# Four graph layers in one kernel: the seams between the passes rearranged

## The chip, the cores and the metric

The kernel runs on one core of one Trainium2 chip. Its time is the device time of one execution in microseconds; the time before is the median of three runs. The engines that matter are TensorE (PE in the profile; its weight loads are PEld), VectorE (DVE), ScalarE (ACT), GpSimd (POOL), SyncE (SP, here only a queue that issues transfers) and the DMA engines. A matmul in fp32 leaves two records in the trace, so four logical matmuls show as eight; a transpose leaves one.

## The reference

The input x has 128 batches of 128 nodes with 256 features, in fp32; adj is one 128 x 128 matrix. Four layers follow one another, each of the form x = x + f(relu(layernorm(x))):

```python
def layer(f, x):
    h = jnp.maximum(_layernorm(x, axis=-1), 0.0)
    return x + f(h)

# f of layer 0: two mixings of h by adj with gates and biases, and a gated loop; relu
# f of layer 1: causal attention within a batch, with adj as the additive mask
# f of layer 2: relu(adj @ (h @ W1)), relu(adj @ (. @ W2)), adj @ (. @ W3)
# f of layer 3:
agg = jnp.einsum('nm,bmd->bnd', A_hat, h)           # A_hat: adj normalised
x   = agg.reshape(-1, d)
z   = _batchnorm(x @ W1.T + b1, g1, be1)            # mean and variance over all 128 x 128 rows
out = jax.nn.relu(z) @ W2.T + b2
out = _batchnorm(out, g2, be2)                      # again over all rows
```

The two batch norms of layer 3 cut the kernel. Nothing after the first can start before the products with W1 of all batches are known, and nothing can be written out before the products with W2 of all batches are known.

## The kernel before

The batches are worked on in 32 groups of four. In the first pass the groups go through layers 0, 1, 2 and the first half of layer 3, staggered: while group g is in layer 2, group g+1 is in layer 1 and group g-1 in layer 3. A string of letters gives the order in which TensorE takes the pieces. The result z of a group (512 KB in two halves) is stored to device memory, but for the last group, which stays in SBUF. The residual x of every group is stored too. The second pass loads z back group by group, applies the first batch norm with relu on ScalarE, and multiplies with W2; the results of all groups stay in SBUF. The output stage applies the second batch norm, turns the result by transposes on TensorE, adds the residual (loaded ahead for some groups) and stores.

Most products are done in seven half-size products instead of eight (`seven`), which needs sums of operand quarters (VectorE) and copies of intermediate results (ScalarE):

```python
def sums(engine, a, extra, s3=None):
    a11, a12, a21, a22 = a
    ...
    engine.tensor_tensor(s1, a21, a22, ALU.add)
    engine.tensor_tensor(s2, s1, a11, ALU.subtract)
    engine.tensor_tensor(s4, a12, s2, ALU.subtract)
    engine.tensor_tensor(s3, a11, a21, ALU.subtract)
    return a11, a12, s4, a22, s1, s2, s3

def seven(product, put, shape, name, pool=None):
    px = bank(shape, f"{name}_x"); product(0, px, True);  t1 = kept(px, 1); yield
    py = bank(shape, f"{name}_y"); product(1, py, True);  put((0, 0), py, t1); yield
    pz = bank(shape, f"{name}_z"); product(4, pz, True);  t5 = kept(pz, 5); yield
    product(5, px, False); t2 = kept(px, 2); yield
    product(2, pz, False); put((0, 1), pz, t2); yield
    product(6, px, False); put((1, 1), px, t5); yield
    product(3, px, False); put((1, 0), px, None); yield
```

Layer 3 of a group in the first pass, and the seam between the passes:

```python
def layer3(g):
    h = norm(g, 3)
    yield
    gT = w.tile([P, DC, T], FP, tag="dT", name=f"gT_{g}", bufs=2)
    mixed(gT, h, ahT, f"pg_{g}", (nc.vector.tensor_copy,))
    ex = ...
    gs = sums(nc.vector, quarters_t(gT), ex)
    yield
    z = ZT[g] = [zp.tile([P, 2, T], FP, tag="z", name=f"zo_{g}_{j}") for j in range(2)]
    done = []

    def put(ij, pb, other):
        i, j = ij
        dst = z[j][:, :, i * T // 2 : (i + 1) * T // 2]
        if other is None:
            nc.scalar.copy(dst, pb)
        else:
            nc.vector.tensor_tensor(dst, pb, other, ALU.add)
        done.append(j)
        if done.count(j) == 2:
            for jj in range(2):
                nc.vector.bn_stats(stats1[:, 2 * j + jj, g, :], z[j][:, jj, :])
            if g != LAST:
                nc.sync.dma_start(Z[g][:, 2 * j : 2 * j + 2, :], z[j])

    yield from seven(columns_by_half(gs, SETS["b"], 0), put, [P, 2, T // 2], f"pz_{g}")

FINAL = "CCCCCCCCCCCCCCCCCCDCCDCCDdDDdDddDdDdddd"   # C: layer 2 of 31, D: layer 3 of 30, d: of 31
...
last1 = bn_part(stats1, FC, slice(LAST - 1, NG), "last1")
awake(60)            # 60 transposes of no use, that keep TensorE's clock up
passA.close()
...
sc1, sh1 = bn_affine(most1, last1, FC, g1_c, be1_c, "bn1", b1_c, 2)
```

`bn_affine` puts together the mean and variance of the first groups and of the last ones and makes a scale and a shift of them; its inverse square root is a power on GpSimd. `norm` takes statistics on VectorE, a power on GpSimd for a whole group, and a relu on ScalarE for each batch. Layer 2 of a group ends with two products `pr`, of two batches each, that are added to x; in layer 3 `mixed` makes the products `pg`.

The second pass and its buffers:

```python
OWN, IN_PASS, IN_Z, ROOM = 6, 8, 14, 19      # residual tiles ahead, by where they lie
...
for n, g in enumerate(ORDER):                # ORDER: the last group first
    ...                                      # relus, sums, seven products of group g
    if n + 1 + AT_ONCE < NG:
        load_z(n + 1 + AT_ONCE)
    if n % 4 == 3 and n // 4 < IN_PASS:
        load_x3(n // 4, nc.sync)
for g in range(IN_PASS, IN_Z):               # in the buffers of z, as they come free
    load_x3(g, nc.sync)
second_pass.close()
late = ...                                   # where the weights and sums of the pass were
for g in range(IN_Z, ROOM):
    load_x3(g, nc.sync)
...
for g in range(NG):
    x3 = R[g]
    for i in range(DC):
        nc.scalar.activation(O[g][:, i, :], O[g][:, i, :], AF.Identity, bias=..., scale=...)
    for q in range(G // 2):
        ...                                  # four transposes
        nc.vector.tensor_tensor(x3[:, half, :], pt, x3[:, half, :], ALU.add)
    nc.sync.dma_start(rows_out[g * P : (g + 1) * P], x3)     # the first and last in halves
    if g + ROOM < NG:
        load_x3(g + ROOM)                    # into a buffer whose store is done
```

Of the kernel before, what the change touches and what calls it, by code (L numbers as in the profile page):

```python
# [15 lines left out]
P = 128  # L16
# [6 lines left out]
def kernel(  # L23
# [55 lines left out]
    psum = ctx.enter_context(tc.tile_pool(name="psum", bufs=8, space=PSUM))  # L79

    def bank(shape, name):
        return psum.tile(shape, FP, tag="bank", name=name)
# [32 lines left out]
    passA = ExitStack()  # L115
# [34 lines left out]
    stats1 = weights.tile([P, FC, NG, 6], FP, name="stats1")  # L150
    stats2 = const.tile([P, DC, NG, 6], FP, name="stats2")
# [123 lines left out]
    def prepare():  # L275
# [57 lines left out]
        yield  # L333
        SETS["b"] = seven_of(bw1T, "bw1T")
# [22 lines left out]
    def norm(g, layer, bs=ALL):  # L357
# [19 lines left out]
        for k, b in enumerate(bs):  # L377
            nc.scalar.activation(  # L378
                h[:, b, :], xt[:, b, :], AF.Relu, bias=sh[:, k : k + 1], scale=rs[:, k : k + 1]
            )  # L380
        return h
# [385 lines left out]
    def layer3(g):  # L767

        h = norm(g, 3)
        yield  # L770
        gT = w.tile([P, DC, T], FP, tag="dT", name=f"gT_{g}", bufs=2)
        mixed(gT, h, ahT, f"pg_{g}", (nc.vector.tensor_copy,))
        ex = w.tile([P, 3, 1, T // 2], FP, tag="ex", name=f"gs_{g}", bufs=2)
        gs = sums(nc.vector, quarters_t(gT), ex)
        yield
# [3 lines left out]
        def put(ij, pb, other):  # L779
            i, j = ij  # L780
            dst = z[j][:, :, i * T // 2 : (i + 1) * T // 2]
            if other is None:
                nc.scalar.copy(dst, pb)
            else:
                nc.vector.tensor_tensor(dst, pb, other, ALU.add)
            done.append(j)
            if done.count(j) == 2:
                for jj in range(2):
                    nc.vector.bn_stats(stats1[:, 2 * j + jj, g, :], z[j][:, jj, :])
                if g != LAST:  # L790
                    nc.sync.dma_start(Z[g][:, 2 * j : 2 * j + 2, :], z[j])

        yield from seven(columns_by_half(gs, SETS["b"], 0), put, [P, 2, T // 2], f"pz_{g}")
# [14 lines left out]
    FINAL = "CCCCCCCCCCCCCCCCCCDCCDCCDdDDdDddDdDdddd"  # L808
# [40 lines left out]
    last1 = bn_part(stats1, FC, slice(LAST - 1, NG), "last1")  # L849
    awake(60)  # L850
    passA.close()

    def bn_affine(most, last, nch, gam, bet, name, bias, n):
# [4 lines left out]
        d = const.tile([P, nch], FP, name=f"d_{name}")  # L858
        nc.vector.tensor_tensor(d, mean1, mean, ALU.subtract)
        nc.vector.scalar_tensor_tensor(mean, d, share, mean, ALU.mult, ALU.add)  # L860
        nc.vector.tensor_tensor(mean, mean, bias, ALU.add)
        nc.vector.scalar_tensor_tensor(d, d, share * (1.0 - share), d, ALU.mult, ALU.mult)
        nc.vector.scalar_tensor_tensor(d, var, 1.0 - share, d, ALU.mult, ALU.add)
        nc.vector.scalar_tensor_tensor(var, var1, share, d, ALU.mult, ALU.add)
        sc = const.tile([P, nch], FP, name=f"sc_{name}")
        inv_sqrt(sc, var, BN_EPS)
        nc.vector.tensor_tensor(sc, sc, gam, ALU.mult)
        sh = const.tile([P, nch], FP, name=f"sh_{name}")
        nc.vector.tensor_tensor(sh, mean, sc, ALU.mult)
        nc.vector.tensor_tensor(sh, bet, sh, ALU.subtract)  # L870
        part = const.tile([P, nch], FP, name=f"part_{name}")
        nc.vector.tensor_tensor(part, bias, sc, ALU.mult)
        nc.vector.tensor_tensor(sh, sh, part, ALU.add)
# [3 lines left out]

    keep = ctx.enter_context(tc.tile_pool(name="keep", bufs=1, reuse_waits="tile"))
    O = [keep.tile([P, DC, T], FP, name=f"o_{g}") for g in range(NG)]


    OWN, IN_PASS, IN_Z, ROOM = 6, 8, 14, 19
    x3p = ctx.enter_context(tc.tile_pool(name="x3p", bufs=OWN, reuse_waits="tile"))
    zin = ctx.enter_context(
        tc.tile_pool(name="zin", bufs=3, side="right", reuse_waits="tile")
    )
# [8 lines left out]
    ORDER = [LAST, *range(LAST)]  # L895
# [8 lines left out]
    def load_x3(g, queue=nc.gpsimd):  # L904
# [5 lines left out]
        else:  # L910
            pool, tag = (x3p, "x3") if k < OWN else (zp, "z") if k < IN_PASS else (late, "x3l")
# [5 lines left out]
    def tell():  # L917

        for g, j in TOLD:
            tc.keep_in_program_order(  # L920
                nc.vector.bn_stats(stats2[:, j, (g + 1) % NG, :], O[g][:, j, :])
            )
        TOLD.clear()
# [4 lines left out]
    def second(g):  # L928

        zl, zr = ZT[g]  # L930
        ex = zw.tile([P, 2, FC // 2, T // 2], FP, tag="zs", name=f"zs_{g}")
# [28 lines left out]
        def put(ij, pb, other):  # L960
            i, j = ij
            dst = O[g][:, j, i * T // 2 : (i + 1) * T // 2]
            if other is None:
                nc.scalar.copy(dst, pb)
            else:
                in_order(dst, pb, other, ALU.add)
            done.append(j)
            if done.count(j) == 2:
                TOLD.append((g, j))
# [13 lines left out]
    for n, g in enumerate(ORDER):  # L983
# [14 lines left out]
        if n % 4 == 3 and n // 4 < IN_PASS:  # L998
            load_x3(n // 4, nc.sync)
    for g in range(IN_PASS, IN_Z):  # L1000
# [5 lines left out]
    late = ctx.enter_context(tc.tile_pool(name="late", bufs=ROOM - IN_Z, side="right", reuse_waits="tile"))  # L1006

    for g in range(IN_Z, ROOM):
        load_x3(g, nc.sync)
    tell()  # L1010
    last2 = bn_part(stats2, DC, slice(LAST, NG), "last2")
    sc2, sh2 = bn_affine(most2, last2, DC, g2_c, be2_c, "bn2", b2_c, 1)
    rows_out = out.rearrange("b (k r) d -> (b k) r d", r=G)
    for g in range(NG):
        x3 = R[g]
        for i in range(DC):
            nc.scalar.activation(
                O[g][:, i, :], O[g][:, i, :], AF.Identity,
                bias=sh2[:, i : i + 1], scale=sc2[:, i : i + 1],
            )  # L1020
        for q in range(G // 2):
            pt = bank([P, 2, D], f"pto_{g}_{q}")
            for r in range(2):
                for i in range(DC):
                    every = O[g][:, i, :].rearrange("c (p r) -> c p r", r=G)
# [45 lines left out]
```

## Time and profile before

| what | before |
|---|---|
| time, median of 3 (lowest to highest) | 2591.45 us (2590.89 to 2592.26) |
| span of the profiled run | 2589.5 us |
| first pass, to the last product with W1 | about 2315 us |
| filler on TensorE between the passes | 60 transposes, 6.7 us |
| second pass, products with W2 | 2321.6 to 2517.8 us |
| output stage, from the first activation | 2522.05 to 2589.5 us |
| moved in all | 143.07 MB |

The profile is one execution. A row of a timeline gives the start in us, the duration, the engine, the line of the kernel, the operation with what it writes and reads, and in square brackets how long the engine had been idle and what ended that. A row of windows gives a stretch of time, and for each engine how long it was busy in it. TensorE counts as busy while it does filler, so its share says little at the seam.

### The profile page before, as it was taken

The numbers are of one execution on the slowest core, as the hardware profiler recorded it, in microseconds if no ns is written. First come the engines' busy times: TensorE is split into PE (matmuls) and PEld (weight loads), VectorE is DVE, ScalarE is ACT, GpSimd is POOL, SyncE is SP. The second block draws the span as 40 slices with busy tenths as digits, with TensorE's granted clock in tenths as the row PEclk, the third lists the DMA queues.
The fourth block names the chain that finished last, engine by engine and source line by source line (L and its number), as shares of the span: only waits on it lengthen the run. The fifth ranks groups of instructions, "written<-read, shape, count | busy, mean of one in ns | idle before, by whom it ended". The sixth has DMA issues, their size and how long they took to land.

```text
span 2589.5 us, 40769 instructions
## 1 busy us (share of the span) xinstructions
PE 2536.8 (98%) x15331; PEld 2292.7 (89%) x15331; DVE 1907.7 (74%) x4788; ACT 1288.9 (50%) x2576; POOL 290.1 (11%) x566
## 2 busy tenths in 40 slices
PE   7999999999999999999999999999999999999996
PEld 5999999999999999999999999999999999888875
DVE  6777777777777777777777777777777776558876
ACT  4544445444444554444444445544454444337766
POOL 1111011111111111011111110111111111000001
PEclk9999999999999999999999999999999999999998
DMA  3000000000000000000000000000000000035559
GB/s 134 15 34 33 33 33 25 25 33 34 33 26 25 33 33 33 33 33 24 26 33 34 33 25 26 33 33 33 34 33 17 34 25 25 25 119 196 171 186 390
DMA packets 49656, 143.07 MB, mean 55 GB/s; under 512 B 4258, under 2 KB 23220, under 8 KB 45492
## 3 DMA queue, kind: packets, MB, share of 16 engines
q1 hardware_dynamic: 42740, 116.81, 12.4%
q0 software_dynamic: 6576, 23.60, 2.5%
q8 instruction: 121, 1.98, 0.3%
q14 instruction: 75, 0.61, 0.1%
q10 hardware_dynamic: 144, 0.07, 0.0%
HBM read 73.48 MB, written 66.98 MB: 54 GB/s over the span
## 4 chain that ended last, share of the span: by engine, by line
PE 94%; DVE 2%; DMA 1%; ACT 1%; POOL 0%; issue 0%; SPq 0%; DVEq 0%; POOLq 0%
PE p_x L446 17%; PE p_x L429 9%; PE p_z L446 8%; PE pmu L401 4%; PE p_z L429 4%; PE pz_x L446 4%; PE p_y L446 4%; PE po_x L951 4%; PE pu_x L429 4%; PE pg L401 2%; PE ps L630 2%; PE pm L555 2%; PE p_y L429 2%; PE pqv_x L587 2%; PE pr L760 2%; PE pz_z L446 2%
## 5 line engine op out<-in xcount | busy, mean ns | idle before, releaser
L378 ACT ACTIVATE h<-x,sh,rs 128x256 f32<-128x256 f32 x512 | 268.9, 589 | 359.3 <-POOL sh L372 349.7
L446 PE MATMUL p_x<-uT,w 128*128 128x256 f32 x1024 | 242.2, 379 | 0.0
L732 ACT ACTIVATE h2T<-h2T 128x512 f32<-128x512 f32 x192 | 120.6, 628 | 230.1 <-DVE h2T L731 230.1
L446 PEld LDWEIGHTS p_x<-uT,w 128*128 128x128 f32 x1024 | 189.7, 190 | 23.2
L363 DVE BATCH_NORM_STATS2 st<-x 128x6 f32<-128x256 f32 x512 | 191.1, 414 | 2.3
L369 POOL TENSOR_SCALAR rs<-mv 128x4 f32<-128x4 f32 x125 | 30.0, 240 | 1351.1 <-ACT h2T L732 1060.7
L513 DVE SCALAR_TENSOR_TENSOR gs<-h,gw 128x256 f32<-128x256 f32 x360 | 151.0, 420 | 27.9 <-ACT h L378 22.6
L461 ACT COPY p_t<-p_x 128x512 f32<-128x512 f32 (+1 forms) x192 | 96.8, 504 | 109.6 <-PE p_x L446 102.8
L370 POOL TENSOR_TENSOR rs<-rs,nhalf 128x4 f32<-128x4 f32 x125 | 145.2, 1161 | 0.0
L401 PEld LDWEIGHTS pmu<-a2T,u 128*128 128x128 f32 x1024 | 119.3, 192 | 14.8 <-issue 14.8
L429 PEld LDWEIGHTS p_x<-w,h2T 128*128 128x128 f32 x1024 | 124.3, 192 | 3.3
L685 ACT ACTIVATE u<-u 128x512 f32<-128x512 f32 x93 | 58.6, 631 | 133.9 <-DVE u L684 133.9
L429 PE MATMUL p_x<-w,h2T 128*128 128x128 f32 x1024 | 124.6, 275 | 0.0
L446 PE MATMUL p_x<-us,w_s 128*128 128x256 f32 x512 | 121.2, 379 | 0.0
L446 PE MATMUL p_x<-uT,w_s 128*128 128x256 f32 x512 | 121.1, 379 | 0.0
L446 PE MATMUL p_z<-us,w 128*128 128x256 f32 x512 | 121.0, 379 | 0.0
L446 PE MATMUL p_z<-us,w_s 128*128 128x256 f32 x512 | 121.0, 379 | 0.0
L446 PE MATMUL p_y<-uT,w 128*128 128x256 f32 x512 | 120.9, 379 | 0.0
L401 PE MATMUL pmu<-a2T,u 128*128 128x128 f32 x1024 | 119.5, 275 | 0.0
L761 DVE TENSOR_TENSOR x<-pr,x 128x512 f32<-128x512 f32 x64 | 43.7, 683 | 90.4 <-PE pr L760 90.4
L446 PEld LDWEIGHTS p_z<-us,w 128*128 128x128 f32 x512 | 97.3, 190 | 13.2
L446 PEld LDWEIGHTS p_z<-us,w_s 128*128 128x128 f32 x512 | 97.3, 190 | 13.2
(317 smaller groups left out, 6174.1 us busy)
## 6 DMA issues: line engine op xcount, KB each, us to landing
z<-zo SPq DMA_DIRECT2D x62, 512.0 KB, 2.6
zi<-z SPq DMA_DIRECT2D x31, 1024.0 KB, 4.9
x<-x POOLq DMA_DIRECT2D x32, 512.0 KB, 3.4
x<-in_x_dram SPq DMA_DIRECT2D x31, 512.0 KB, 4.1
out_dram<-x3i SPq DMA_DIRECT2D x30, 512.0 KB, 12.1
x3i<-x SPq DMA_DIRECT2D x19, 512.0 KB, 5.2
x3i<-x POOLq DMA_DIRECT2D x13, 512.0 KB, 11.1
w<-in_L_gnn_W_dram SPq DMA_DIRECT2D x1, 2048.0 KB
```

Source lines behind the costliest of these rows:

```text
L363: nc.vector.bn_stats(st[:, k, :], xt[:, b, :])
L370: nc.gpsimd.tensor_tensor(rs, rs, nhalf[:, :n], ALU.pow)
L378: nc.scalar.activation(h[:, b, :], xt[:, b, :], AF.Relu, bias=sh[:, k : k + 1], scale=rs[:, k : k + 1])
L401: nc.tensor.matmul(pm[:, k, :], src[:, b, c * P : (c + 1) * P], aT, start=True, stop=True)
L429: nc.tensor.matmul(pb[:, rr, :], a_r[r][:, c, rr * P : (rr + 1) * P], b_r[r][:, c, :wide], start=(first and rr == 0 and c == 0), stop=(c = ...
L446: nc.tensor.matmul(pb[:, jj, :], b_r[r][:, c, at : at + P], a_r[r][:, c, :], start=(first and jj == 0 and c == 0), stop=(c == nk - 1), ski ...
L461: nc.scalar.copy(t, pb)
L513: nc.vector.scalar_tensor_tensor(gs, h[:, b, :], 1.0, gw[:, i, :], ALU.mult, ALU.mult, accum_out=gl[:, k, i : i + 1],)
L555: nc.tensor.matmul(pm[:, r, :], cmbT[:, b, :], h[:, b, :], start=True, stop=True)
L685: nc.scalar.activation(dst, dst, AF.Relu)
L732: nc.scalar.activation(dst, dst, AF.Relu)
L951: nc.tensor.matmul(pb, BW2R[r][:, c, :], a_r[r][:, c, :], start=(first and c == 0), stop=(c == FC // 2 - 1), skip_group_check=True,)
```

## The change

It has five parts. The last group goes through layer 3 in two halves of two batches, each with a norm of its own (the power of two batches is asked for by VectorE), and its product with W1 is a plain one of four blocks, without sums and kept copies; its statistics, and those of the group before it, are taken for each half block, straight from PSUM where the result is not a sum. The last word of the order string moves one piece of group 30 behind layer 2 of group 31. `bn_affine` is written so that fewer steps lie before and after the power. The last result of the second pass stays in PSUM, which sets free 4 KB per partition for one more residual tile; the sums of the second pass get buffers that the residuals can take over while the pass still runs; nine residuals instead of eight are loaded within it. And the relus of the second group in layer 0 are pinned behind the instructions that come before them in the program. What it is for: a shorter way from the last product of one pass to the first of the next, fewer loads left for the output stage, and a start without a blocked queue.

```diff
+    passA = ExitStack()
+    psum = [passA.enter_context(tc.tile_pool(name="psum", bufs=8, space=PSUM))]
...
+    bw1T_12 = weights.tile([P, F1 // 2], FP, name="bw1T_12")
...
+        nc.scalar.copy(bw1T_12, bw1T[:, 0, F1 // 2 :])
         SETS["b"] = seven_of(bw1T, "bw1T")
...
-            nc.scalar.activation(
+            relu = nc.scalar.activation(
                 h[:, b, :], xt[:, b, :], AF.Relu, bias=sh[:, k : k + 1], scale=rs[:, k : k + 1]
             )
+            if (g, layer) == (1, 0):
+                tc.keep_in_program_order(relu)
...
     def layer3(g):
-        h = norm(g, 3)
-        yield
-        gT = w.tile([P, DC, T], FP, tag="dT", name=f"gT_{g}", bufs=2)
-        mixed(gT, h, ahT, f"pg_{g}", (nc.vector.tensor_copy,))
-        ...
+        parts = [ALL] if g < LAST else HALVES
+        for bs in parts:
+            h = norm(g, 3, bs)
+            yield
+        gT = tile_of(g, parts[0], [P, DC, T], "dT", f"gT_{g}", 2)
+        for i, bs in enumerate(parts):
+            mixed(gT, h, ahT, f"pg_{g}_{i}", (nc.vector.tensor_copy,), bs)
+            if g < LAST:
+                ...  # sums, as before
+            yield
...
         def put(ij, pb, other):
+            if other is not None:
+                nc.vector.tensor_tensor(dst, pb, other, ALU.add)
+            if g >= LAST - 1:
+                at = 2 * g - LAST + 1 + i
+                for jj in range(2):
+                    nc.vector.bn_stats(
+                        stats1[:, 2 * j + jj, at, :], (pb if other is None else dst)[:, jj, :]
+                    )
             if other is None:
                 nc.scalar.copy(dst, pb)
...
+        if g < LAST:
+            yield from seven(columns_by_half(gs, SETS["b"], 0), put, [P, 2, T // 2], f"pz_{g}")
+            return
+        for i, j in (0, 0), (1, 0), (0, 1), (1, 1):
+            pb = bank([P, 2, T // 2], f"pz_{g}_{i}_{j}")
+            for jj in range(2):
+                for c in range(DC):
+                    ...  # b: weights of block j, jj, chunk c
+                    nc.tensor.matmul(pb[:, jj, :], b, gT[:, c, i * T // 2 : (i + 1) * T // 2], ...)
+            put((i, j), pb, None)
+            yield
...
-    FINAL = "CCCCCCCCCCCCCCCCCCDCCDCCDdDDdDddDdDdddd"
+    FINAL = "CCCCCCCCCCCCCCCCCCDCCCCDDdDDddDdDdDdddd"
...
-    awake(60)
+    awake(41)
...
     def bn_affine(most, last, nch, gam, bet, name, bias, n):
+        nc.vector.tensor_scalar(var, var, 1.0 - share, BN_EPS, ALU.mult, ALU.add)
         nc.vector.tensor_tensor(d, mean1, mean, ALU.subtract)
+        nc.vector.scalar_tensor_tensor(var, var1, share, var, ALU.mult, ALU.add)
+        nc.vector.scalar_tensor_tensor(e, d, share * (1.0 - share), d, ALU.mult, ALU.mult)
+        nc.vector.tensor_tensor(var, var, e, ALU.add)
+        inv_sqrt(sc, var, 0.0)
         nc.vector.scalar_tensor_tensor(mean, d, share, mean, ALU.mult, ALU.add)
         nc.vector.tensor_tensor(mean, mean, bias, ALU.add)
-        ...  # four steps, inv_sqrt, and six steps
+        nc.vector.tensor_tensor(d, bias, mean, ALU.subtract)
         nc.vector.tensor_tensor(sc, sc, gam, ALU.mult)
+        nc.vector.tensor_tensor(sh, d, sc, ALU.mult)
+        nc.vector.tensor_tensor(sh, sh, bet, ALU.add)
...
-    OWN, IN_PASS, IN_Z, ROOM = 6, 8, 14, 19
+    psum.append(... tc.tile_pool(name="psum2", bufs=6, space=PSUM, reuse_waits="tile"))
+    last_o = ... tc.tile_pool(name="last_o", bufs=1, space=PSUM, reuse_waits="tile")
+    # O[ORDER[-1]]: two tiles of last_o; the other results in SBUF as before
+    OWN, IN_PASS, IN_Z, IN_ZS, ROOM = 7, 9, 15, 17, 20
+    zsp = ctx.enter_context(tc.tile_pool(name="zsp", bufs=2, side="right", reuse_waits="tile"))
...
-        ex = zw.tile([P, 2, FC // 2, T // 2], FP, tag="zs", name=f"zs_{g}")
+        ex = zsp.tile([P, 2, FC // 2, T // 2], FP, tag="zs", name=f"zs_{g}")
...  # put of the second pass, for the last group only:
+            told = stats2[:, j, LAST + i, :]
+                if last:
+                    tc.keep_in_program_order(nc.vector.bn_stats(told, pb))
                 nc.scalar.copy(dst, pb)
+                if last:
+                    TOLD.append((told, dst))     # statistics of the half, taken a step later
...
-        if n % 4 == 3 and n // 4 < IN_PASS:
-            load_x3(n // 4, nc.sync)
-    for g in range(IN_PASS, IN_Z):
+        if n % 3 == 2 and n // 3 < IN_PASS:
+            load_x3(n // 3, nc.sync)
+    for g in (9, 10, 15, 11, 12, 16, 13, 14):
         load_x3(g, nc.sync)
...
-    for g in range(IN_Z, ROOM):
+    for g in range(IN_ZS, ROOM):
         load_x3(g, nc.sync)
```

## The prediction

> **What bounds the kernel now.** I read the page first, then the timeline wherever TensorE is not back to back, then short windows of the end.
>
> ```profile
> PE 2536.8 (98%) x15331; PEld 2292.7 (89%) x15331; DVE 1907.7 (74%) x4788; ACT 1288.9 (50%) x2576; POOL 290.1 (11%) x566
> PE 94%; DVE 2%; DMA 1%; ACT 1%; POOL 0%; issue 0%; SPq 0%; DVEq 0%; POOLq 0%
> ```
>
> TensorE is on 94% of the chain that ended last, so what the change can win lies in the gaps of TensorE: the start, the seam between the two passes, the end. The start, from the timelines of ScalarE and TensorE (start, duration, instruction, what ended the idle time):
>
> ```profile
> 36.21 1.09 ACT L378 ACTIVATE h<-x,sh,rs 128x256 f32<-128x256 f32 x2 [3.64 <-POOL sh L372]
> 37.21 0.35 ACT L394 COPY hT<-pt 128x256 f32<-128x256 f32 x1
> 37.61 2.08 PE L606 MATMUL pqv<-hT,m_qk 128*128 128x256 f32 x4 [4.44 <-ACT hT L394]
> 40.92 1.03 PE L606 MATMUL pqv<-hT,m_qk 128*128 128x256 f32 x4
> 44.69 0.40 ACT L643 ACTIVATE p<-p,nmax 128x128 f32<-128x128 f32 x1 [1.68 <-DVE nmax L640]
> ```
>
> Two relus of group 1 stand in ScalarE's queue ahead of the copy of hT and wait for GpSimd until 36.21. The copy is blocked behind them, and TensorE with it for 4.44 us; its next four matmuls then take twice their usual time. The seam, from the timeline of all engines:
>
> ```profile
> 2297.09 1.88 PE L760 MATMUL pr<-s,a2T 128*128 128x512 f32 x4
> 2303.79 2.07 ACT L378 ACTIVATE h<-x,sh,rs 128x256 f32<-128x256 f32 x4 [1.61 <-POOL sh L372]
> 2315.06 6.71 PE L108 MATMUL awake<-ident 128*128 128x128 f32 x60
> 2315.88 1.29 DVE L789 BATCH_NORM_STATS2 stats<-zo 128x6 f32<-128x512 f32 x2 [0.28 <-ACT zo L783]
> 2318.76 1.01 POOL L221 TENSOR_TENSOR sc_bn<-sc_bn,nhalf 128x4 f32<-128x4 f32 x1 [15.00 <-DVE sc_bn L219]
> 2320.66 2.93 ACT L939 ACTIVATE zo<-zo,sh_bn,sc_bn 128x512 f32<-128x512 f32 x4 [4.81 <-DVE sh_bn L873]
> 2321.61 1.32 PE L951 MATMUL po_x<-zo,bw2T 128*128 128x256 f32 x4
> ```
>
> From the last real product (end about 2315.1) to the first of the second pass (2321.6), TensorE only does filler. The end, in windows (busy time of PE, PEld, DVE, ACT, POOL; then clock, DMA share, GB/s):
>
> ```profile
> 2512.00:2516.00 4.00, 3.91 (x18) 2.74 (x16) 3.96 (x8) 0.75 (x2) 0.00 (x0) 1.00 0.78 266
> 2516.00:2520.00 4.00, 1.32 (x5) 0.68 (x4) 3.08 (x12) 0.37 (x1) 0.00 (x0) 1.00 0.28 72
> 2520.00:2524.00 4.00, 1.09 (x4) 0.70 (x5) 1.06 (x8) 1.96 (x3) 0.70 (x1) 0.76 1.00 372
> 2580.00:2584.00 4.00, 0.00 (x0) 0.00 (x0) 0.00 (x0) 0.00 (x0) 0.00 (x0) 0.50 1.02 419
> 2584.00:2588.00 4.00, 0.00 (x0) 0.00 (x0) 0.00 (x0) 0.00 (x0) 0.00 (x0) 0.50 0.58 227
> ```
>
> The last compute instruction ends at about 2572, yet the DMA engines are full from 2520 to 2586. The end is bound by bytes: it is set by how much has still to move when the second pass frees its buffers.
>
> **What the Trainium skill says.** "TensorE: Matmul & The Clock Gate", Part 1, says that an idle window of about 3.4 us halves TensorE's clock; the trace agrees (2.08 against 1.03 us after the 4.44 us gap). "PSUM — Partial Sum Buffer", Engine vs sequencer instructions, says that ScalarE's and VectorE's queues are strict FIFO: that is the blocked copy. The same page, PSUM bank collisions, says that two engines may not touch one bank and partition quadrant at once, reads included; in the changed program each ScalarE copy of a PSUM result accordingly waits for VectorE's statistics of it. No run so far shows what that costs. "DMA: Bandwidth & Descriptors", Issuing engines are not separate DMA queues, says that all queues share 16 engines; the trace has share 1.02 at 419 GB/s whichever queue issues.
>
> **The change part by part.** I compared the order of instructions per engine. Between the first 80 us and the last group nothing moves but one added ScalarE copy of 128x256 (0.37 us beside full matmuls, 0). Times below are on the clock of before.
>
> *Start.* The copy of hT now comes before all four relus. Its transposes end at 33.2, VectorE's half of the copy at 34.1, so the projections run from about 34.1, warm, to 37.2 (1.76 us for each of two blocks; the first matmul is earlier). But the four relus still wait for 36.2, end at 38.3, and now the copy of qv stands behind them: 38.9. Then the exp table (1.28) and the first exp at 40.25 instead of 44.69. The exps gate the rest, so the gain is 4.4, kept to the end because TensorE is full from there.
>
> *Seam, removed.* pr_0 is issued before the last product of layer 2: 2294.45 instead of 2297.09. The norm of the first half follows: add 2295.5, two statistics and aggregates to 2297.25, power on GpSimd to 2298.2, relus 2298.45 to 2299.5 (before: all four from 2303.79). The second half still hangs on pr_1 (2298.8): add 2299.7, statistics 2300.7, power 2301.6, relus 2301.85 to 2304.05 with two copies between them. So pg of half 0 is not waited for, and pg of half 1 hardly.
>
> *Seam, added.* The plain product is 16 logical matmuls instead of 14; at two records each of 0.216 us (a product of 14 takes 6.04 us, 28 records) that is 0.86 us more on TensorE. TensorE from pr_0: pr 1.76, the layer-2 product 1.79, seven products of group 30 6.04, pg 1.79, plain blocks 6.90, sum 18.3, and about 1.0 of waiting (pr_1 waits for a ScalarE copy): end at 2313.7, 1.35 earlier.
>
> *Seam, the statistics.* Read from PSUM at 0.42 us each, they end 1.05 after the last product, at 2314.75 (before: copy, then 1.29 us of statistics, 2317.17). Aggregates to 2315.1; four small operations instead of six before the power (0.7) 2315.85; power 1.1; 2316.95; three after it 0.6; relu 2317.6; first product at its usual 0.9 later: 2318.5 instead of 2321.6. Seam: 3.1. ScalarE's copies, held by the statistics and by the store of group 30's z (2.6 us to landing), end about 2315.4, two us ahead of the relu. The filler, 41 x 0.109 (6.55 / 60) = 4.5 us, ends at 2318.2 and delays nothing.
>
> *Second pass.* 6.04 us per group of 28 records, as before; six PSUM banks are two groups of three. 0.
>
> *End of the pass, added.* VectorE gets one statistics of a half (0.37), one scaling (0.17) and a second half statistics (0.36) ahead of the add that releases the last product: that product starts 0.9 later and ends at 2518.75. After it, statistics from PSUM 0.4, aggregate 0.2, four operations 0.7, power 0.8, three 0.6: first output activation at 2521.45, 0.6 earlier than 2522.05. That is not what counts; the start of the last loads is.
>
> *Loads.* Before, 8 residual tiles are loaded in the pass, 4 at its end, 7 once it is over, 13 into reused buffers: after the pass 20 loads and 32 stores of 0.524 MB, 27.3 MB, which at 412 GB/s is 66.2 us: 2520 to 2586. After: 9 in the pass, 6 at its end (two in buffers of the sums), 5 once it is over, 12 reused: 49 instead of 52 transfers. 3 x 0.524 / 0.419 = 3.75 us less, 0.9 later: 2.85.
>
> Sum: 4.4 + 3.1 + 2.85 = 10.35; 2591.45 - 10.35 = 2581.1.
>
> **The rivals.** (a) *The end stays bound by bytes but starves at its beginning*: five loads instead of seven bridge the time to the first store. They last 7 us from 2520.2, the first store comes at 2524.7 (3.25 after the first activation, as before), so for is the arithmetic, against it that ScalarE gives one group per 1.41 us, 372 GB/s, under the 419. Cost up to 1 us: 2582. (b) *A late VectorE eats the seam*: statistics of half blocks are more instructions (0.42 twice against 0.69), and copies wait for them. VectorE has 2 us spare there; if not, 1 to 2 us of the 3.1 are lost: 2583. (c) *The wait at the start only moves*: the relus now delay qv. I have that in; were the exps not the gate, the gain would be the 3.5 us of hT alone: 2582. (d) *More than counted*: if the end of the pass doesn't slip by 0.9: 2580.
>
> **Range and chances.** The parts are independent and each is uncertain by about 1 us, the end by 1.5; all three are wins in working and none is large. Range 2578.0 to 2585.5. 2% is 52 us, far outside: faster 0.01, same 0.985, slower 0.005.
>
> **What would show it.** In the changed profile: no idle of 4 us ahead of the projection at 34, no slow matmuls there, exp at 40.2; filler of 41 followed by po_x within 0.5 us, 7.5 us (4.4 + 3.1) before 2321.6; DMA share at 1 from the end of the pass for about 62.5 us. Wrong would be: a shift at 100 us under 3.5, a relu of the seam that waits for something other than the last statistics, or DMA share under 0.9 within the end.

## The result and the profile after

| | before | after |
|---|---|---|
| time, median (lowest to highest) | 2591.17 us (2590.89 to 2592.26) | 2582.2 us (2580.38 to 2582.89) |
| ratio to before | | 0.9964, 95% interval 0.9946 to 0.9981 |
| span of the profiled run | 2589.5 us | 2581.1 us |

The kernel is 9.0 us faster; the interval of the ratio makes that 4.9 to 14.0 us. 2581.1 was predicted, with a gain of 10.35. A second measurement of the same kernel, further down, gave 0.9971. The page of the profile after (busy time of each engine; then the shares of the chain that ended last):

```profile
PE 2535.9 (98%) x15316; PEld 2293.4 (89%) x15316; DVE 1905.8 (74%) x4795; ACT 1288.8 (50%) x2577; POOL 288.9 (11%) x563
PE 95%; ACT 2%; DVE 1%; DMA 1%; issue 0%; POOL 0%; SPq 0%; DVEq 0%; POOLq 0%
```

Nothing of the 8.4 us between the two spans is visible there: TensorE is busy for 0.9 us less and no share of the chain moves by more than a point. The places have to be read one by one. The start, in the timelines of TensorE and ScalarE after (start, duration, instruction, what ended the idle time before it):

```profile
30.97 2.08 PE L612 MATMUL pqv<-hT,m_qk 128*128 128x256 f32 x4
36.13 0.37 ACT L400 COPY hT<-pt 128x256 f32<-128x256 f32 x1 [0.42 <-PE pt L398]
36.56 1.13 PE L612 MATMUL pqv<-hT,m_qk 128*128 128x256 f32 x4 [0.24 <-ACT hT L400]
37.21 2.08 ACT L381 ACTIVATE h<-x,sh,rs 128x256 f32<-128x256 f32 x4 [0.70 <-POOL sh L375]
42.18 0.41 ACT L649 ACTIVATE p<-p,nmax 128x128 f32<-128x128 f32 x1 [1.12 <-DVE nmax L646]
```

The order is the one the pin asks for. The copy of hT is no longer behind the relus, TensorE waits 0.24 us for it where it waited 4.44, and the four relus come after it. But the first exp is at 42.18, only 2.51 us ahead of before, and the slow projection (2.08 us) has not gone: it now comes first, at 30.97. The seam, from the timeline of all engines after:

```profile
2292.28 1.02 PE L766 MATMUL pr<-s,a2T 128*128 128x512 f32 x2
2296.68 1.09 ACT L381 ACTIVATE h<-x,sh,rs 128x256 f32<-128x256 f32 x2 [1.18 <-DVE sh L378]
2306.15 5.34 PE L820 MATMUL pz<-gT,bw1T 128*128 128x256 f32 x24
2311.33 4.64 PE L109 MATMUL awake<-ident 128*128 128x128 f32 x41
2311.53 0.76 DVE L798 BATCH_NORM_STATS2 stats<-pz 128x6 f32<-128x256 f32 x2 [0.96 <-PE pz L820]
2312.32 0.59 ACT L802 COPY zo<-pz 128x512 f32<-128x512 f32 x1 [0.41 <-DVE stats L798]
2314.95 2.93 ACT L983 ACTIVATE zo<-zo,sh_bn,sc_bn 128x512 f32<-128x512 f32 x4 [2.04 <-DVE sh_bn L902]
2316.07 1.15 PE L995 MATMUL po_x<-zo,bw2T 128*128 128x256 f32 x4
```

From the start of the filler to the first product of the second pass there are 4.74 us, where there were 6.55. The last statistics end 0.96 us after the last product, the relu of the second pass waits for the last step of the shift on VectorE, and the copies that had to wait for the statistics (0.41 us the last one) end at 2312.91, two us before the relu. The end, in windows (PE, PEld, DVE, ACT, POOL; then clock, DMA share, GB/s):

```profile
2512.00:2516.00 4.00, 1.04 (x4) 0.59 (x4) 2.46 (x14) 0.61 (x2) 0.70 (x1) 0.84 0.48 132
2516.00:2520.00 4.00, 3.39 (x15) 3.01 (x16) 1.36 (x3) 4.00 (x7) 0.00 (x0) 0.50 1.02 401
2524.00:2528.00 4.00, 3.45 (x24) 2.89 (x23) 3.89 (x8) 4.00 (x7) 1.65 (x3) 1.00 1.00 310
2572.00:2576.00 4.00, 0.00 (x0) 0.00 (x0) 0.00 (x0) 0.00 (x0) 0.00 (x0) 0.50 1.03 420
2576.00:2580.00 4.00, 0.00 (x0) 0.00 (x0) 0.00 (x0) 0.00 (x0) 0.00 (x0) 0.50 0.50 195
```

The DMA engines are full from 2516 to about 2578, while the last compute instruction is done well before: it is still bytes that set the end.

To compare traces that are shifted against each other, I read six marks in each: VectorE's first use of a weight matrix w that it has to wait for, the last product pm of group 0's layer 0 before group 1 starts (near 26 us), the first product pmu (near 130), the first po_x of the second pass, the last po_x of it, and the end. The first two columns are times from the start of the span, each of the next four is the distance to the mark before it, in us:

| kernel | w used | pm | pm to pmu | pmu to po_x | to the last po_x | to the end | span |
|---|---|---|---|---|---|---|---|
| before | 12.58 | 25.05 | 106.54 | 2190.02 | 195.10 | 72.8 | 2589.5 |
| after | 13.62 | 26.94 | 102.28 | 2186.85 | 195.84 | 69.2 | 2581.1 |
| after, again | 13.95 | 26.80 | 103.55 | 2186.85 | 195.85 | 69.3 | 2582.4 |
| without the pin | 13.91 | 27.21 | 105.89 | 2187.27 | 195.85 | 68.5 | 2584.7 |
| pin alone | 13.84 | 26.64 | 103.57 | 2190.28 | 195.10 | 72.7 | 2588.3 |
| last group whole, filler 60 | 14.06 | 27.27 | 102.23 | 2191.14 | 194.62 | 69.2 | 2584.5 |
| last group whole, filler 41 | 13.36 | 27.07 | 103.42 | 2189.46 | 195.55 | 69.0 | 2584.5 |
| two tiles fewer | 14.08 | 26.55 | 101.91 | 2187.23 | 195.85 | 71.6 | 2583.1 |
| statistics after the add | 14.50 | 27.55 | 102.08 | 2186.77 | 195.41 | 69.8 | 2581.6 |
| and early aggregate | 13.80 | 26.35 | 101.41 | 2187.29 | 193.90 | 69.8 | 2578.7 |
| without late loads | 14.46 | 27.80 | 102.28 | 2186.76 | 195.84 | 55.6 | 2568.3 |
| warm start | 14.47 | 27.61 | 102.05 | 2188.48 | 194.69 | 69.0 | 2581.8 |
| early aggregate, warm start | 14.39 | 27.90 | 102.10 | 2187.10 | 194.10 | 69.9 | 2581.1 |
| early aggregate, weights first | 14.01 | 27.02 | 102.04 | 2186.76 | 194.45 | 69.4 | 2579.7 |

Between before and after, 3.17 us go at the seam (3.1 predicted), 3.6 at the end (3.75 predicted), the pass grows by 0.74 (0.9 predicted). Of the 4.4 at the start the trace shows 4.26 from pm on, but pm itself is 1.89 us later than before. That is the question which the experiments had to settle.

### The profile page after: what moved, and what is told of

It reads as the page before. It is cut to its first block, busy times and chain, and to the rows that moved or that the text cites. A ratio compares the mean times of both kernels' runs of the same rounds, so it can differ in the third digit from the quotient of the medians.

```text
span 2581.1 us, 40737 instructions
## 1 busy us (share of the span) xinstructions
PE 2535.9 (98%) x15316; PEld 2293.4 (89%) x15316; DVE 1905.8 (74%) x4795; ACT 1288.8 (50%) x2577; POOL 288.9 (11%) x563
## 4 chain that ended last, share of the span: by engine, by line
PE 95%; ACT 2%; DVE 1%; DMA 1%; issue 0%; POOL 0%; SPq 0%; DVEq 0%; POOLq 0%
PE p_x L452 17%; PE p_x L435 9%; PE p_z L452 8%; PE pmu L407 4%; PE p_z L435 4%; PE p_y L452 4%; PE po_x L995 4%; PE pu_x L435 4%; PE pz_x L452 4%; PE pg L407 2%; PE pm L407 2%; PE ps L636 2%; PE pm L561 2%; PE p_y L435 2%; PE pr L766 2%; PE pqv_x L593 2%
## 5 line engine op out<-in xcount | busy, mean ns | idle before, releaser
L452 PEld LDWEIGHTS p_y<-uT,w 128*128 128x128 f32 x512 | 97.2, 190 | 13.2
```

Of the source, the lines that this page charges most:

```text
L452: nc.tensor.matmul(pb[:, jj, :], b_r[r][:, c, at : at + P], a_r[r][:, c, :], start=(first and jj == 0 and c == 0), stop=(c == nk - 1), ski ...
```

## The experiments

### The pin, taken out of the new kernel and put alone into the old one

```diff
 # new kernel without the pin
-            if (g, layer) == (1, 0):
-                tc.keep_in_program_order(relu)
 # old kernel with the pin alone
+            if (g, layer) == (1, 0):
+                tc.keep_in_program_order(relu)
```

> The changed kernel without the pin of the relus of group 1. Theory (blocked queue): ScalarE's copy of hT waits again behind two relus, TensorE is idle for 4 to 4.5 us ahead of the projection and runs its next matmuls at half speed; from the end of the transposes to the first exp 11.5 us as before instead of 5.9; time 2582.2 + 4.4 = 2586.6. Rival (the start gained only what the two traces differ by at the end of the first pass, 2.2 us, because the exps or the loads gate it anyway): 2584.4.

> The kernel before with the pin alone. Theory: from the transposes to the first exp 5.9 us instead of 11.5, at least 4.4 of it kept: 2591.2 - 4.4 = 2586.8; the end of the first pass and all that follows moves by the same amount. Rival: 2591.2 - 2.2 = 2589.0.

Without the pin: 2586.69 us, ratio 0.9977 (0.9968 to 0.9985). The pin alone: 2588.84 us, ratio 0.9988 (0.9981 to 0.9994), which is 3.1 us (1.6 to 4.9). Put beside the two measurements of the new kernel (0.9964 and 0.9971), taking the pin out costs 1.6 to 3.4 us. In the traces it gives, from pm to pmu, 2.97 us in the old kernel, and 3.61 or 2.34 in the new one, whose two traces differ. So all of this lies near 3, under the 4.4 that the trace of before suggests, though the interval of the sole use does not exclude 4.4. The timeline without the pin tells why (ScalarE and TensorE):

```profile
37.48 1.10 ACT L381 ACTIVATE h<-x,sh,rs 128x256 f32<-128x256 f32 x2 [1.49 <-POOL sh L375]
38.88 1.13 PE L609 MATMUL pqv<-hT,m_qk 128*128 128x256 f32 x4 [2.29 <-ACT hT L397]
46.16 0.41 ACT L646 ACTIVATE p<-p,nmax 128x128 f32<-128x128 f32 x1 [2.93 <-DVE nmax L643]
```

Here the same two relus block the same copy, but TensorE loses 2.29 us to it instead of 4.44, where 4 to 4.5 was expected. Both ends of the wait have moved. Counted from pm, the transposes begin at 8.75 us instead of 7.50, since the first of the projections ahead of them ran at half clock (2.08 us instead of 1.13), and the relus come at 10.27 instead of 11.16, since GpSimd was done earlier with the shift that they wait for. So part of the wait in the trace of before is time that another execution spends ahead of it. There are only two traces without the pin, so how often each case comes stays open.

That the exps gate the rest is shown: from the first exp to pmu it takes 86.9 to 87.1 us in 12 of the 14 traces, with the pin and without it.

### Where the start varies

A weight matrix w of layer 2 is asked for by the same instruction in all kernels. Its first use on VectorE, before:

```profile
12.58 0.43 DVE L239 TENSOR_TENSOR w_s<-w 128x256 f32<-128x256 f32 x1 [2.38 <-DMA w<-in_L_gnn_W_dram]
```

and after:

```profile
13.62 0.43 DVE L241 TENSOR_TENSOR w_s<-w 128x256 f32<-128x256 f32 x1 [3.00 <-DMA w<-in_L_gnn_W_dram]
```

In 13 traces that use lies between 13.36 and 14.50; only in that of before at 12.58, though the old kernel with the pin alone, which issues the same loads in the same order, has 13.84. The trace that the prediction was read from had the earliest of all. VectorE's sums of w stand in its queue ahead of a copy of h0T, for which TensorE waits (0.42 us in before, 1.03 in after), and through it the layer goes on to pm: again a queue that is blocked by its first instruction. The first product pm of the layer starts 4.1 us after this use in every trace. To move these sums back was not tried. The unaltered new kernel was measured again to see how far two executions of one program lie apart:

> The changed kernel again, unaltered, beside the others. Theory (what the first trace of it lost at the start, 2.2 us against the 4.4 that I predicted, is TensorE's clock and the loads of that run, and the blocked queue costs 3 us on average): the landmark pmu of group 1 at 128.6 to 130.4, as in the three other pinned kernels, against 131.8 and 133.3 without the pin; time 0.9964 of before, within 0.001. Rival (a loss that belongs to the change): pmu at 129.4 within 0.2 every time.

2583.36 us, ratio 0.9971 (0.9960 to 0.9981); in the traces, pmu comes at 129.22 in one and 130.35 in the other (128.6 to 130.4 expected), and from there to the first po_x both take 2186.85 us. What differs between these two lies in the first 130 us, and not in w or in pm (26.94 and 26.80), but between pm and pmu: 102.28 and 103.55.

### The clock at the start

TensorE is idle for 1.47 us ahead of the first transposes of group 1, and the first projection after them takes 2.08 us in most of the traces, 1.13 in a few, with the same program. The experiment puts 12 transposes of no use there:

```diff
-    FILL = "aacaaccacapcabpccpbdbdAdbd..."
+    FILL = "aacaaccacapcabpccpwbdbdAdbd..."     # w: awake(12)
```

> The kernel after with 12 transposes of no use on TensorE ahead of group 1's first transposes near 29 us, so that TensorE is not idle there. My theory, that the first projections at 31 us run at half clock in most executions (2.08 instead of 1.03 to 1.13 us) because of the short idle times before them: they run at full clock, the transposes of the second pair end near 34 us in every execution, and the first product with the adjacency of group 1 comes at 127.9 to 128.7 us as in the two earlier runs that were warm; 1 to 1.5 us faster than the kernel after, near 2581.5. Rival, that the filler itself holds up the transposes, or that the variation comes from the landing of the first loads: no gain, the product at 129.5 to 130.5.

2582.47 us, ratio 0.9964 (0.9951 to 0.9978): no different from the new kernel. The timeline of TensorE shows that the filler did what it was to do:

```profile
28.57 1.47 PE L109 MATMUL awake<-ident 128*128 128x128 f32 x12
31.49 1.13 PE L612 MATMUL pqv<-hT,m_qk 128*128 128x256 f32 x4 [0.24 <-ACT hT L400]
```

The projection is fast, yet from pm to pmu the kernel takes 102.05 us, and the new kernel with its slow projection 102.28; pmu comes at 129.66, as the rival said. pm, ahead of the filler, is late (27.61), because w is (14.47), and after it the relus wait for GpSimd.

But the clock is not out of it: what half clock costs depends on how long it lasts. In the first trace of the new kernel the granted clock was 0.50 from 30 to 32 us, 0.68 from 32 to 34 and 1.00 from 34 to 50, and of the first products of this kind only one took 2 us. In the second trace it was 0.50 from 30 to 36 us, and the rows of TensorE and ScalarE there are:

```profile
34.40 1.85 PE L612 MATMUL pqv<-hT,m_qk 128*128 128x256 f32 x4
37.40 0.37 ACT L400 COPY hT<-pt 128x256 f32<-128x256 f32 x1 [1.18 <-PE pt L398]
```

The copy waits for the transposes behind the slow projections, and the relus behind the copy no longer wait for GpSimd. Counted from pm, the first exp comes at 16.65 us instead of 15.24, and pmu 1.27 us later. The pin alone shows the same: clock 0.50 from 30 to 34 us and 0.54 to 36, first exp at 16.63, pmu at 103.57. In the two kernels with the filler the exp comes at 15.01 and 14.30. So a short stretch at half clock is hidden behind GpSimd, and a long one costs some 1.3 us. Whether the filler pays on average the times do not tell: the traced execution of the kernel with it also lost time at the seam, as shown further down.

### The last group: two parts against one

```diff
-        parts = [ALL] if g < LAST else HALVES
+        parts = [ALL]                       # sums and seven products for the last group too
...
-    FINAL = "CCCCCCCCCCCCCCCCCCDCCCCDDdDDddDdDdDdddd"
+    FINAL = "CCCCCCCCCCCCCCCCCCDCCDCCDdDDdDddDdDdddd"
-    awake(41)
+    awake(60)                               # in the second of the two: 41, as in the new kernel
```

> The changed kernel, but the last group goes through layer 3 whole and with seven half-size products and sums again, the order string and the filler of 60 as before; statistics of half blocks from PSUM, the shorter scale and shift, the loads and the pin stay. Theory: of the 3.4 us that the traces show for the seam, 0.9 is the shorter scale and shift (2.36 us from the last aggregate to the relu instead of 3.24), so 2.5 are lost: 2584.7. Rival (the plain product gives back what the halves win, and the statistics from PSUM are the gain): under 1 us lost, 2583.

> The changed kernel with the last group whole and in seven products again, as in the run before with 60 pieces of filler, but with the changed kernel's 41. Theory (the filler of 60 held TensorE 2 us after the relu was done): the first product of the second pass follows the relu by 0.9 to 1.1 us, and the kernel is 2.7 us slower than the changed one (the relu came 2.7 us later from the landmark pmu) instead of 4. Rival (the filler doesn't matter): as slow as with 60.

With 60 transposes: 2586.18 us, 0.9977 (0.9967 to 0.9986). With 41: 2585.47 us, 0.9976 (0.9968 to 0.9984). In the first of them the timeline of TensorE and ScalarE shows two things at once:

```profile
2314.09 6.71 PE L109 MATMUL awake<-ident 128*128 128x128 f32 x60
2317.95 2.94 ACT L983 ACTIVATE zo<-zo,sh_bn,sc_bn 128x512 f32<-128x512 f32 x4 [2.27 <-DVE sh_bn L902]
2320.64 1.03 PE L995 MATMUL po_x<-zo,bw2T 128*128 128x256 f32 x4
```

The relu starts 3.86 us after the filler does with the whole group, 3.62 with halves (2311.33 to 2314.95), so little of the difference is behind the last product; most is that the last product ends earlier with halves. From pmu to the relu the whole group takes 2188.45 us and the halves 2185.73: 2.7 us. And a filler of 60 is now too long: it ends at 2320.8, so the first product comes 2.69 us after the relu, where the new kernel has 1.12. With 41 the relu is at 2318.54, 2188.05 us after pmu, or 2.3 more than with halves; the first product follows it after 1.41 us and not 0.9 to 1.1, since it waited 0.64 for its weights.

These 2.3 to 2.7 us are what halves and plain product gain over a whole group whose statistics are also taken per half block. They are not their share of the change: in these two kernels the last product ends later after pmu (2184.59 and 2184.19 us) than in before (2183.47). The two traces of before and after split the 3.34 us from pmu to the relu (2189.07 to 2185.73) directly. The last product ends 1.36 earlier (2182.11). From it to the end of the last aggregate it takes 1.26 us instead of 2.36, as the statistics are taken per half block and no longer wait for a copy: 1.10. From there to the relu it takes 2.36 instead of 3.24, the shorter scale and shift: 0.88. The last aggregates on VectorE, before and after:

```profile
2317.09 0.33 DVE L799 BATCH_NORM_AGGREGATE mv_last<-stats 128x2 f32<-128x12 f32 x2
2312.21 0.38 DVE L831 BATCH_NORM_AGGREGATE mv_last<-stats 128x2 f32<-128x24 f32 x2
```

A late first product is not a late pass. With the filler of 60 the first product comes 1.68 us later after pmu than with 41 (2191.14 and 2189.46), the last one only 0.75 later (2385.76 and 2385.01, the sums of two columns); the ratios of the times are nearly the same.

### Two residual tiles fewer

```diff
-    OWN, IN_PASS, IN_Z, IN_ZS, ROOM = 7, 9, 15, 17, 20
+    OWN, IN_PASS, IN_Z, IN_ZS, ROOM = 7, 9, 15, 15, 18
-    for g in (9, 10, 15, 11, 12, 16, 13, 14):
+    for g in (9, 10, 11, 12, 13, 14):
```

> The changed kernel with 18 residual tiles ahead instead of 20: the two in the buffers of the sums are left out, so 51 instead of 49 transfers remain once the second pass is over. Theory (the end is bound by bytes): DMA share at 1 to the end, 2 x 1.25 = 2.5 us longer: 2584.7. Rival (ScalarE, at 1.41 us for each group, bounds the end, or the stage starves at its beginning): under 0.8 us, 2583 at most.

2585.2 us, 0.9973 (0.9962 to 0.9985). From the last product to the end it takes 71.6 us instead of 69.2: 2.4, for 2 x 0.524 MB, or 1.2 us for each tile, which is 437 GB/s with the rounded 2.4 (windows of the end show 420). The three of the change gave 3.6, the same 1.2 each. Its last windows have the whole difference in them:

```profile
2576.00:2580.00 4.00, 0.00 (x0) 0.00 (x0) 0.00 (x0) 0.00 (x0) 0.00 (x0) 0.50 0.98 396
2580.00:2584.00 4.00, 0.00 (x0) 0.00 (x0) 0.00 (x0) 0.00 (x0) 0.00 (x0) 0.50 0.11 37
```

### No loads in the output stage

```diff
         if g + ROOM < NG:
-            load_x3(g + ROOM)
+            R[g + ROOM] = R[g]              # the residual of the last 12 groups is left out
```

> The kernel after without the 12 residual loads of the output stage that go into reused buffers: groups 20 to 31 add the tile that lies in the buffer, so the residual of the last 12 groups is left out of the result, and 6.3 MB fewer are moved. My theory, that the end is bound by bytes: 12 x 0.524 / 0.415 = 15 us less to move, more than the end can use; it then runs at ScalarE's pace, 32 groups of 1.41 us = 45.3 us from the first output activation, and some 6 us for the last group to be turned, added and stored: about 51 us after the first activation instead of 65.3, so 13 to 14 us faster than the kernel after, near 2569. Rival, that the end is bound by ScalarE and VectorE and their buffers already: within 2 us of the kernel after.

2569.83 us, 0.9918 (0.9904 to 0.9931): 12.4 to 13.5 us under the two measurements of the new kernel. The first output activation is at 2516.51 and the span ends at 2568.3, 51.8 us later. A window of the stage shows the change of bound, DMA share under 1 and ScalarE busy all the time:

```profile
2544.00:2548.00 4.00, 3.45 (x24) 2.88 (x24) 3.63 (x7) 4.00 (x7) 0.00 (x0) 1.00 0.94 371
```

So the bytes of these loads are worth 13 us, and a residual tile that finds room earlier pays until about eleven more have been moved (13 / 1.2, an estimate); then ScalarE, with 45.18 us for its 64 activations, is the bound.

### The last statistics of the second pass

In the new kernel the last product of the second pass waits for 1.43 us (0.52 before):

```profile
2511.91 1.13 PE L995 MATMUL po_x<-zi,bw2s_late 128*128 128x256 f32 x4 [1.43 <-DVE o L970]
```

Two steps were to take this back: the half statistics are taken just ahead of the copy of the last product instead of one step earlier, and, in the second kernel, the two long aggregates of 186 values are taken one and two groups earlier, so that they are not in VectorE's queue there.

```diff
-                    TOLD.append((told, dst))
+                    HELD.append((told, dst))         # taken just ahead of the last product's
...
 # in the second kernel also
-            if k == 0 and n + 1 == NG:
-                most2 = bn_part(stats2, DC, slice(LAST), "most2")
+            if k == 0 and n in (NG - 3, NG - 2):
+                ...                              # some: 29 groups, of one half of the features
+                tc.keep_in_program_order(nc.vector.bn_aggr(mv2[:, j, :], some))
...
-    last2 = bn_part(stats2, DC, slice(LAST, NG + 1), "last2")
+    last2 = bn_part(stats2, DC, slice(LAST - 2, NG + 1), "last2")
```

> The changed kernel, but the statistics of the half blocks of the last result are taken behind the add that releases the last product, not ahead of it. Theory (VectorE's order sets the end of the pass): TensorE's idle time ahead of the last product falls from 1.43 to 0.5 to 0.7 us, the last loads start 0.8 us earlier and the end comes 0.8 us earlier. Rival (the start of the loads doesn't set the end): the idle time falls, the end stays within 0.3 us of the pass's first product plus 264.4.

> As the run before, and the two aggregates over 186 values (0.98 us each) are made one and two groups earlier, over 29 groups, so that none lies in the last group. Theory: no idle time of TensorE over 0.4 us in the last group, the last product 1.9 to 2.3 us earlier relative to the pass's first product than in the changed kernel, the end 1.5 to 2.3 us earlier. Rival (VectorE is at 83% in the pass and an aggregate of 0.98 us stalls TensorE where it is put): the last product at most 1 us earlier.

The first: 2582.58 us, 0.9967 (0.9955 to 0.9980). The wait fell only to 0.99, not to 0.5 to 0.7, the last product came 0.43 us earlier after the pass's first, and the end came no earlier (265.2 us after the first product, 265.0 in the new kernel): the theory missed. The second: 2580.67 us, 0.9961 (0.9947 to 0.9976). The last product in it:

```profile
2508.95 1.13 PE L995 MATMUL po_x<-zi,bw2s_late 128*128 128x256 f32 x4 [0.53 <-DVE o L970]
```

It waits as little as in before, and the pass is 1.94 us shorter than in the new kernel (195.84 to 193.90; 1.9 to 2.3 expected). 0.44 of that is a later first product; from pmu to the last product it is 1.50 (2382.69 to 2381.19). And the end is 0.6 us longer; one window of it says where that is lost:

```profile
2524.00:2528.00 4.00, 3.47 (x24) 2.99 (x24) 3.64 (x7) 4.00 (x7) 1.08 (x2) 1.00 0.88 308
```

The DMA engines are not full here. The loads into reused buffers wait until the tile that lies there has been filled and stored: GpSimd's queue, which issues them, stands for 4.26 us ahead of the fifth. It does so for 3.98 ahead of the sixth in the new kernel too, so that this is the cause of the difference is not shown. It would be rival (a) of the prediction, and it takes back 0.6 of the 1.5 us that the pass gains. The intervals of the ratios overlap almost wholly. Measured side by side, all four executions of the second kernel (2579.86 to 2581.53) were below all eight of the new one (2581.60 to 2584.44), but the first measurement of the new one (2580.38 to 2582.89) reaches into them, so a gain is likely, but not shown.

### The last combinations

Both steps with the warm start; and both steps with the load of the weights bw2T put ahead of the load of the second group's z at the seam:

```diff
+    nc.sync.dma_start(bw2T, BW2T)
     load_z(1)
-    nc.sync.dma_start(bw2T, BW2T)
```

> The kernel after with the statistics of the last result taken ahead of its copies in the step before, with the long aggregate of the second pass taken two steps earlier in two parts (both as in the earlier run with the early aggregate, 2580.67), and with the 12 transposes of no use at the start. If the two gains add up: 1 to 1.5 us under that run, near 2579.3. If the filler at the start gives nothing: 2580 to 2581.

> The kernel of the run with the early aggregate (2580.67), with one pair of loads swapped at the seam: the weights bw2T of the second pass are asked for ahead of the 1 MB of z of its second group. In three of the kernels so far the first product of the second pass waited for these weights (0.64, 0.45 and 1.83 us). If the weights are a second way into the seam, nearly as long as the statistics: the first product comes 1.1 us after the relu, without a wait for a DMA, and the median is 0.3 to 1 us under the earlier run, 2579.7 to 2580.4. If the z of the second group then comes late instead: a wait of TensorE or ScalarE for zi near 2322, and no gain.

The first gave 2582.52 us, 0.9966 (0.9953 to 0.9978), above both of its expectations, so no gain of the filler at the start is shown, as with it alone. In its trace pm is the latest of all (27.90), and the clock was 0.52 from 48 to 50 us. The second gave 2581.13 us, 0.9961 (0.9948 to 0.9975). It was tried because of a row like this one, of the kernel with the warm start:

```profile
2318.14 1.10 PE L995 MATMUL po_x<-zo,bw2T 128*128 128x256 f32 x4 [1.83 <-DMA bw2T<-BW2T]
```

There the relu had begun at 2315.28, and the weights came 1.83 us after TensorE could have started. Three traces show such a wait (0.45, 0.64 and 1.83 us). With the weights first there was none, po_x 1.12 us after the relu, but the median is no better than that of the kernel without the swap. The table says why: in the three kernels with the early aggregate the first product comes 2187.29, 2187.10 and 2186.76 us after pmu, the last one 2381.19, 2381.20 and 2381.21. A first product up to half a microsecond late is caught up within the pass; of the 1.63 us that the kernel with the warm start is late, 0.48 is left at the last product (2383.17 against 2382.69). So the weights are not a second way into the seam unless they come very late; how often they do stays open. The kernel with the early aggregate and its variant with the weights first have the lowest ratio of those that leave nothing out (0.9961), within the uncertainty of the new kernel.

## Why the prediction came out as it did

*The time.* 2581.1 was predicted, 2582.2 measured, inside the range; the gain is 9.0 and, measured again, 8.1 us, against 10.35. Four of its five terms held (seam, second pass, slip, loads), and one was too large.

*Start.* This is the term that was mis-sized: "the exps gate the rest, so the gain is 4.4, kept to the end". The mechanism is right: the exps gate. In the two traces, counted from pm, the first exp is 4.40 us earlier (19.64 to 15.24) and pmu 4.26. But the prediction named as a sign of its being wrong a shift at 100 us under 3.5, and the shift of the two traces is 2.37 (131.59 to 129.22). The 1.89 that are missing are the later pm: 1.04 is the later use of w, the rest lies in the weight products between 19 and 24 us, which took 4.73 us in after and 3.83 in before. The old kernel with the pin alone has a late pm too (26.64), so nothing points to the change; but there is only one trace of before. The measure of the pin itself is its removal and its sole use: about 3 us, where 4.4 was put into the sum. The step that failed was to take the wait of one trace for the wait of the kernel. In that trace the projections ahead of the wait ran at full clock, and GpSimd's shift came late after pm; in the other trace without the pin the wait was 2.29 us. "Warm" held for the projections it was said of (1.13 us at 36.56), but the first projection of the pair ahead of them, 1.13 us in the trace of before, took 2.07 to 2.08 in 9 of the 12 traces without filler, and where half clock lasted until 36 us it delayed the exps by 1.4. So the 4.26 of the first trace after is itself a lucky case; the second has 2.99. Rival (c), that the wait only moves and the gain is 3.5, said 2582, which was met by luck: it asks that the exps not be the gate, and they are.

*Seam.* 3.1 predicted, 3.17 in the traces to the first product, and 3.34 to the relu: 1.36 from the earlier last product (1.35 predicted), 1.10 from the statistics, 0.88 from the scale and shift. The last statistics end 0.96 after the last product (1.05 predicted), the copies two us ahead of the relu as predicted. On the cost of the shared bank, left open there: the Trainium skill, "PSUM — Partial Sum Buffer", PSUM bank collisions, says that two engines must not be on the same part of one bank at once; the copies wait 0.41 to 0.65 us for the statistics, and none of it is on the path. Rival (b) did not happen. The filler of 41 delays nothing; one of 60 would have put the first product 1.8 us later (6.55 - 4.74, an estimate), and the last one less, as the whole group shows.

*End of the pass and loads.* The slip of 0.9 measured 0.74 to the last product, rival (d) did not happen. The three tiles measured 3.6 against 3.75, and the two taken away 2.4 against 2.5 (2 x 0.524 / 0.419): bytes, as read. "DMA share at 1 for about 62.5 us" is 2516 to 2578. Rival (a), starvation at the beginning, shows in the window 2524 to 2528, 310 GB/s, but before has two such windows of 372 and 373; measured from the last product it does not cost the new kernel more than a tenth or two. It begins to cost when the pass ends earlier, as in the kernels with the early aggregate.

## What to carry to other kernels

A wait in a trace is one sample: before its length goes into a sum, look at what sets both of its ends, and whether the work ahead of it ran at full clock there; another execution may spend part of the wait on that work. Compare stretches from a mark behind the first loads, and take a second trace of the same program to see how far the stretch itself varies (1.27 us here). When a stage is bound by bytes, multiply the bytes by the rate of that stage and nothing else; here that held to 0.2 us for two and three tiles, and for twelve up to the pace of the next engine. And after a seam has been shortened, look again at what was hidden by its old length, the filler and the first loads into reused buffers; but judge it at the end of the next pass and not at its first product, since that pass may catch up.

## What the runs showed of the hardware

The same stretch of the same program ran at half clock in some executions and at full clock in others: the first projection of group 1 took 2.07 to 2.08 us in the new kernel, both times, and 1.13 us in two kernels whose start is the same (two tiles fewer; early aggregate), after the same idle time of 1.47 us. How long half clock lasted varied as well: the granted clock was 0.50 until after 32 us in one execution of the new kernel, until 36 in the other. The Trainium skill, "TensorE: Matmul & The Clock Gate", Part 1, says that the window in which activity is counted runs freely and that the place of the change varies between runs; the traces agree, and an idle time well under the 3.4 us named there was enough, with the sparse work around it. With twelve transposes in the gap, 1.47 us, the clock stayed up in both kernels that had them; it did so in 3 of the 12 traces without them too, so two traces are few.

The first use of the same weights, asked for by the same instruction, varied by 1.9 us between the traces (12.58 to 14.50), and pm by 2.85 us (25.05 to 27.90). That is about as much as one part of the change brings.
